# A macaron block on one core: two quarters of the heads in one step of values, tile work placed beside tile work, the last linear as a line of its own

## The chip, the core and the metric

The kernel runs on one core of a Trainium2 chip. The metric is the device time of one execution in microseconds; three runs of the kernel before took 934.36 to 934.98, with a median of 934.62. The engines named below are TensorE (PE for its matmuls, PEld for its loads of weights), VectorE (DVE), ScalarE (ACT), GpSimd (POOL) and SyncE (SP, a DMA queue). Everything is in fp32 but for one masking product in bf16.

## What is computed

The input x has 16 batches of 256 tokens with 128 features. Six sublayers follow, each adding to x; `ln` is a layer norm.

```python
x = x + 0.5 * ffn(ln(x))          # layer 0
x = x + nonlocal_attn(ln(x))      # layer 0, no softmax
x = x + 0.5 * ffn(ln(x))          # layer 0, the same weights
x = x + 0.5 * experts(ln(x))      # layer 1: x + sum over 2 of 8 rank-64 experts, gated by token 0
x = x + attention(ln(x))          # layer 1: 16 heads of 8, rotary, causal softmax
x = x + 0.5 * experts(ln(x))      # layer 1

def ffn(x):                       # all weights ternary with a scale per output
    h = silu(x @ w1) * (x @ w2)   # 128 -> 512
    h = gelu(h @ h1); h = gelu(h @ h2)   # 512 -> 512
    return h @ w3                 # 512 -> 128
```

## The kernel before

The batches are split into nine groups: seven of two batches (four tiles of 128 tokens) and two of one. Everything stays on the chip between the first load of x and its store.

**The planner.** The order of instructions is made while the program is built. Each piece of work is a generator, a *line*, that yields steps; a step (L235 `step`) has an engine, a guessed duration, the PSUM banks and buffers that it takes and drops, the keys that it needs and those that it sets. `begin` (L1004) works out when the next step of a line could start on the planner's clocks; the loop at L1137 takes the earliest, gathers those of the same engine that could start within SLACK of it, and issues the first by a key (L1143): on TensorE the main line comes last while `back` is true (L1142: until the last HURRY feed-forwards have begun), and first after that; then by rank. `issue` (L1053) emits the step's instructions; each engine then runs its own list in that order and waits at semaphores. On TensorE, `issue` adds SWITCH to the guess where `tiles` changes, and `awake` puts matmuls of the identity by itself into waits, but only after `ended` is set. A softmax's exponential is held back by PATIENCE (L1016) while ACT has another function's table loaded. `ended` also decides between two forms of the layer norm (L306) and between masking the scores on VectorE or by TensorE (L769).

**Main line.** `feed_forwards` (L1108) runs the 18 feed-forwards one after another, (0, g) being the group's first and (1, g) its second, in the order of L1103; the last three are (0, 8), (1, 7), (1, 8). After (0, g) it spawns the nonlocal attention, after (1, g) the chain experts, attention, experts. When the last feed-forward has issued its last step, `ended` is set (L1126). A feed-forward (`ffn`, L281) is two products with the 512-wide first linears, two 512 x 512 linears as seven half-size products each (a Strassen form with sums on DVE and POOL, at L478), and the last linear with w3s (L521 to L540), whose steps are part of the main line.

**Attention.** The 16 heads lie in four quarters j of four heads, one in each 32-row strip of the array. For a batch, `maxima` (L760) takes the row maxima of the scores; `weighted` (L825) then, for j in 0, 2, 1, 3, computes scores again (a block of matmuls on 32 rows each, "row" tiles, tile name `pb<-qkv`), spawns `softmax` (an exponential on ACT into one of three buffers `pr`, then two selects on POOL that clear the masked half), and the values line (L881) multiplies by V and a column of ones: a block of 16 matmuls into 32 columns each ("col" tiles, `pb<-pr,vm`), which frees its `pr`. In a block four matmuls run side by side, and it is one step of the planner. In the last two groups (`late`) the two halves of the heads have an output each; otherwise one output follows the fourth quarter.

Of the kernel before, what the change touches and what calls it, by code (L numbers as in the profile page):

```python
# [20 lines left out]
P = 128  # L21
# [6 lines left out]
LANDING = 2.2  # L28
LOAN = 1.5
SPARED = 0.5  # L30
PATIENCE = 1.5
HURRY = 1
SLACK = 0.02
HOP = {"PE": 0.24, "ACT": 0.15, "DVE": 0.12, "POOL": 0.08}
SWITCH = 0.1
# [22 lines left out]
def macaron_kernel(ctx: ExitStack, tc: tile.TileContext, a: dict, out: bass.AP):  # L58
# [316 lines left out]
    def ffn(which, t0, n):  # L375
# [77 lines left out]
            add_residual(t0 + i * n // 2, n // 2, po)  # L453

        for c in range(KC):
            r = yield pe(0.215 * n, banks=1, after=0.0, take=("h",) if c == 0 else ())
            h = r[1] if c == 0 else h
            pu = r[0]
            nc.tensor.matmul(pu.t[:, :N], w1T[:, c * P : (c + 1) * P], xnT.t[:, :N], start=True, stop=True)
            sil = sml.tile([P, TG], F32, name="sil", bufs=3)  # L460
            spawn(silu(c, pu, sil))
            (pw,) = yield pe(0.215 * n, banks=1, after=0.0, drop=(xnT,) if c == KC - 1 else ())
            nc.tensor.matmul(pw.t[:, :N], w2T[:, c * P : (c + 1) * P], xnT.t[:, :N], start=True, stop=True)
            spawn(product(c, pw, sil, h))
            if me == (0, 0) and c == 1:
                fold_w3()
        lo, hi = 0, 2 * P
        for l, w in ((1, h1T), (2, h2T)):
            wx, T = extra[l - 1], {}

            def rest(l=l, h=h, T=T):
                yield from sums(l, h, T)

            spawn(rest())
            bk = {}
            nh = None

            for p, b, first, at, second, needs in (  # L478
                (1, "a", w[:, 0:2], lo, (0, 0), has(l, 0, 0) + (("A11", l),)),
                (5, "d", w[:, 0:2], hi, 1, (("T", 1, l, me), ("A", l))),  # L480
                (6, "b", wx[:, 0], 0, 2, (("T", 2, l, me),)),
                (7, "c", wx[:, 1], 0, 3, (("T", 3, l, me),)),
                (2, "a", w[:, 2:4], lo, (1, 0), has(l, 1, 0) + (("P1", l, me),)),
                (3, "d", wx[:, 2], 0, (1, 1), has(l, 1, 1) + (("V", l, me),)),
                (4, "c", w[:, 2:4], hi, 4, (("T", 4, l, me), ("C22", l, me))),
            ):
                new = p in (1, 5, 6, 7)
                for o in range(2):
                    for k in range(2):
                        begins, ends = o + k == 0, o + k == 2  # L490
                        drop = ()
                        if ends and p in (5, 7, 4):
                            drop = (T[{5: 1, 7: 3, 4: 4}[p]],) + ((h,) if p == 4 else ())
                        r = yield pe(
                            0.1075 * n, banks=int(new and begins), after=0.0, take=("h",) if p == 1 and begins else (),
                            needs=needs, drop=drop, sets=(("P6", l, me),) if p == 6 and ends else (),
                        )
                        if new and begins:
                            bk[b] = r[0]
                        if p == 1 and begins:  # L500
                            nh = r[1]
                        src = block(h, *second) if type(second) is tuple else T[second].t[:, :, :M]
                        nc.tensor.matmul(
                            in_two(bk[b])[:, o, :], first[:, k, at + o * P : at + o * P + P], src[:, k, :],
                            start=new and begins, stop=p in (2, 3, 4, 6) and k == 1, skip_group_check=True,
                        )
                if p == 1:
                    spawn(left(l, bk["a"], nh))
                elif p == 6:
                    spawn(shared(l, bk["b"], bk["d"], nh))  # L510
                elif p == 7:
                    spawn(last_block(l, bk["c"], nh))
                elif p == 2:
                    spawn(gelu(l, 0, 0, in_two(bk["a"]), block(nh, 0, 0), drop=(bk["a"],)))
                elif p == 3:
                    spawn(other_block(l, 0, 1, bk["d"], nh))
                elif p == 4:
                    spawn(other_block(l, 1, 0, bk["c"], nh))
            h = nh

        half = n // 2  # L521
        po = {}
        up, down = (0, 1, 2, 3), (2, 3, 0, 1)
        for t, ks in [(t, down) for t in range(half, n)] + [(t, up) for t in range(half)]:
            new = t in (0, half)
            last = t in (half - 1, n - 1)
            r = yield pe(
                0.225 * len(ks), banks=int(new), after=0.0, needs=tuple((2, i, t // half, me) for i in range(2)),
                drop=(h,) if t == half - 1 else (),
            )  # L530
            if new:
                po[t // half] = r[0]
            b = po[t // half]
            for k in ks:
                nc.tensor.matmul(
                    b.t[:, t % half * P : (t % half + 1) * P], h.t[:, k, t * P : (t + 1) * P], w3s[:, k, :],
                    start=(k == ks[0]), stop=(k == ks[-1]),
                )
            if last:
                spawn(residual(t // half, b))  # L540


    eye, tri = (wgT[:, i * P // 2 : (i + 1) * P // 2].bitcast(BF16) for i in range(2))
# [8 lines left out]
    def nonlocal_attn(t0, n):  # L552
# [17 lines left out]
            copy(m[:, :nb], pp[:, :nb])  # L570
            return m

        gram = yield from product(0.45 * nb, None, None, "gram", (xn,))
        m = yield from product(0.22 * nb, gram, pht, "gph")
        m = yield from product(0.22 * nb, m, wgT, "eff")
        if t0 == 2 * FIRST[NG - 1]:
            spawn(for_the_mask())
        (po,) = yield pe(0.45 * nb, banks=1, drop=(xnT,))
        for t in range(n):
            nc.tensor.matmul(  # L580
                po.t[:, t * D : (t + 1) * D], xnT.t[:, t * P : (t + 1) * P], m[:, t // 2, :], start=True, stop=True
# [4 lines left out]

    def gated(nb, cls):

        (bk,) = yield pe(0.22 * nb, banks=1)
        pl = bk.t[:, : nb * NE].rearrange("p (b e) -> p b e", e=NE)  # L590
        for b in range(nb):
            nc.tensor.matmul(pl[:, b, :], cls[:, b, :].to_broadcast([P, P]), wrT, start=True, stop=True)
# [32 lines left out]
        (bk,) = yield pe(0.23 * nb, banks=1, drop=(ab,))  # L625
# [12 lines left out]
    def applied(key, sg, xnT):  # L638
        yield step(None, 0.0, needs=(key,))
        we = merged[key]  # L640
        (po,) = yield pe(0.225 * sg.n, banks=1, drop=(we, xnT) if sg.last else (xnT,))
# [61 lines left out]
    def attention(sg):  # L703
# [5 lines left out]
        xnT = yield from by_feature(n, xn)  # L709
        if sg.first:  # L710

            (bk,) = yield pe(0.22 * nb, banks=1)
# [32 lines left out]

        spawn(keys())
        spawn(queries())
        (bk,) = yield pe(0.225 * n, banks=1, needs=(("q", sg.t0),), drop=(xnT,))
# [76 lines left out]
        def weighted(i):  # L825
# [55 lines left out]
            def values():  # L881

                po = [None, None]
                for j in (0, 2, 1, 3):
                    new = j == 0 or (late and j == 1)
                    yield step(None, 0.0, needs=(("pr", sg.t0, i, j), ("v", sg.t0)))
                    pr = prs[j]
                    r = yield pe(0.025 + 0.00174 * o, banks=int(new), tiles="col", drop=(pr,))
                    if new:
                        po[j % 2 :] = [r[0]] * (2 - j % 2)  # L890
                    half = slice((j % 2) * w, (j % 2) * w + w)
                    pp = po[j % 2].t[:, half]
                    for k, f, at in runs:
                        for r in range(4):
                            nc.tensor.matmul(
                                pp[32 * r : 32 * r + 32, (f - q0) * P :], vm.t[:, base // P + k, r, j, :],
                                pr.t[:, r, at : at + (q1 - f) * P],
                                start=(j < 2 and k == 0), stop=(j >= 2 and k == q1 - 1), skip_group_check=True,
                            )
                    if late and j >= 2:  # L900
                        spawn(output(pp, oT[:, half], w // 32, j % 2, po[j % 2], ("oT", sg.t0, i, j)))
# [206 lines left out]
    def feed_forwards():  # L1108

        for which, sg in order:  # L1110
# [12 lines left out]
                spawn(chain(experts(sg), attention(sg), after_attention(sg)), (1, sg.g))  # L1123
            if (which, sg) == order[0]:
                fold_rest()
        ended[0] = True  # L1126

    def told(*key):
# [8 lines left out]
    while lines:  # L1137
# [2 lines left out]
        engine = min(ready, key=lambda r: r[:2])[2].next["engine"]  # L1140
        soon = [r for r in ready if r[0] <= t + SLACK and r[2].next["engine"] == engine]
        back = engine == "PE" and begun[0] <= len(order) - HURRY  # L1142
        line = min(soon, key=lambda r: ((r[2] is main) == back, r[2].rank, r[1]))[2]  # L1143
        issue(line)
        if line.over:
            lines.remove(line)
# [69 lines left out]
```

## Time and profile before

| | us |
|---|---|
| median of three runs | 934.62 |
| profiled execution, device time | 934.55 |
| its span on the core | 932.8 |
| PE busy | 904.2 (6524 matmul records) |
| DVE busy | 636.3 |
| ACT busy | 471.5 (110.3 of it 86 loads of tables) |
| POOL busy | 356.4 |
| granted TensorE clock | 0.996 |

The span runs from the first to the last instruction; the device time holds a little more. An fp32 matmul is two records (two passes). In the profile all kernel instructions carry line 227, that of the helper which records them, so groups are told apart by their tiles: `pb` is PSUM, `w3s` the last linear's weights, `T`, `h`, `hS`, `h1T` and `h2T` belong to the 512 x 512 linears, `qkv` to scores, `pr,vm` to values, `ident` alone to the filling matmuls, `wgT` alone (bf16) to the mask on TensorE. A shape such as 128\*32 is rows by columns of the array that a matmul uses.

### The profile page before, as it was taken

What the parts mean: (1) busy time and instruction counts of PE and PEld (TensorE: products, weight loads), DVE (VectorE), ACT (ScalarE), POOL (GpSimd) and SP (SyncE); (2) the same over time, 40 slices, a digit from 0 to 9 for tenths busy, and PEclk for the clock granted to TensorE, in tenths of its full rate; (3) what the DMA queues carried; (4) which work ended last, traced back from release to release, by engine and by line L of the source; (5) the groups of instructions that cost most, each with busy time, mean ns of one, the idle gap of its engine ahead of it and who ended that gap; (6) DMA issues with size and microseconds to landing.
All of it is one profiled execution on the core that took longest, in us unless ns stands there. A gap on an engine that the chain in (4) does not pass through costs nothing.

```text
span 932.8 us, 16458 instructions
## 1 busy us (share of the span) xinstructions
PE 904.2 (97%) x6524; PEld 680.5 (73%) x6524; DVE 636.3 (68%) x1474; ACT 471.5 (51%) x691; POOL 356.4 (38%) x537
## 2 busy tenths in 40 slices
PE   6999999999999999999999999999999989999998
PEld 4778778686786767787677767866786767877666
DVE  4744646875488485894678764894778586977773
ACT  2233533645754646546555466547574657465332
POOL 5311313522454334442453324532463246443441
PEclk9999999999999999999999999999999999999999
DMA  8100000000000000000000000000000000000000
GB/s 240 33 1 1 1 1 12 12 1 1 13 12 12 1 2 12 24 1 1 12 1 24 1 1 13 24 1 1 13 2 23 1 12 1 25 7 2 13 19 12
DMA packets 14588, 13.68 MB, mean 15 GB/s; under 512 B 2032, under 2 KB 11952, under 8 KB 14512
## 3 DMA queue, kind: packets, MB, share of 16 engines
q1 hardware_dynamic: 12496, 8.04, 3.0%
q0 software_dynamic: 1600, 4.20, 1.6%
q8 instruction: 51, 0.84, 0.4%
q10 hardware_dynamic: 416, 0.39, 0.1%
q14 instruction: 25, 0.20, 0.1%
HBM read 10.53 MB, written 2.10 MB: 14 GB/s over the span
## 4 chain that ended last, share of the span: by engine, by line
PE 70%; DVE 14%; ACT 6%; issue 4%; POOL 2%; DMA 2%; SPq 1%; POOLq 0%; DVEq 0%
PE pb L227 70%; DVE mx L227 4%; DVE h L227 3%; ACT L227 2%; ACT pr L227 2%; DVE pb L227 2%; DMA w3s<-in_w3T_dram 1%; ACT h L227 1%; POOL pr L227 1%; DVE T L227 1%; DMA x<-in_x_dram 1%; DVE st L227 1%; DVE qkv L227 1%; POOL rstd L227 1%; DVE row L227 0%
## 5 line engine op out<-in xcount | busy, mean ns | idle before, releaser
L227 DVE TENSOR_TENSOR h<-h,pb 128x512 f32<-128x512 f32 (+1 forms) x180 | 111.7, 620 | 80.8 <-PE pb L227 78.8
L227 PE MATMUL pb<-T,hS 128*128 128x256 f32 (+1 forms) x576 | 131.8, 364 | 3.9 <-DVE h L227 2.8
L227 POOL TENSOR_SCALAR_AFFINE_SELECT pr<-pr 128x512 f32<-128x512 f32 x128 | 78.8, 639 | 140.4 <-ACT pr L227 135.3
L227 ACT ACTIVATE h<-h 128x512 f32<-128x512 f32 (+1 forms) x108 | 62.3, 581 | 137.7 <-DVE h L227 137.3
L227 ACT ACTIVATE pr<-pb 128x1536 f32<-128x1536 f32 x64 | 92.7, 1449 | 54.0 <-PE pb L227 40.4
L227 PE MATMUL pb<-qkv 32*128 32x256 f32 (+2 forms) x1536 | 115.2, 406 | 4.7 <-ACT pr L227 2.5
L227 ACT ACT_TABLE_LOAD x86 | 110.3, 1283 | 17.8 <-PE pb L227 15.5
L227 DVE TENSOR_REDUCE mx<-pb 128x8 f32<-128x2048 f32 (+1 forms) x64 | 111.9, 1750 | 6.1 <-PE pb L227 5.7
L227 PEld LDWEIGHTS pb<-T,hS 128*128 128x128 f32 x576 | 96.5, 190 | 21.1 <-issue 8.6
L227 DVE TENSOR_TENSOR pb<-pb,causal 128x1024 f32<-128x1024 f32 x56 | 68.7, 1226 | 45.4 <-PE pb L227 37.3
L227 PEld LDWEIGHTS pb<-qkv 32*128 32x128 f32 x1536 | 68.0, 184 | 38.3 <-issue 11.4
L227 ACT ACTIVATE xn<-x,shift,rstd 128x128 f32<-128x128 f32 x138 | 57.1, 482 | 52.9 <-POOL shift L227 52.7
L227 POOL TENSOR_SCALAR nm<-mv 128x4 f32<-128x4 f32 (+3 forms) x56 | 14.8, 264 | 168.3 <-DVE mv L227 167.1
L227 POOL TENSOR_TENSOR T<-h 128x512 f32<-128x512 f32 (+1 forms) x48 | 53.4, 1112 | 58.9 <-ACT h L227 54.9
L227 POOL TENSOR_TENSOR T<-h,T 128x512 f32<-128x512 f32 (+1 forms) x40 | 46.1, 1151 | 64.9 <-DVE h L227 35.0
L227 PE MATMUL pb<-xnT,w1T 128*128 128x512 f32 (+1 forms) x144 | 68.9, 560 | 0.9 <-ACT xnT L227 0.9
L227 PE MATMUL pb<-xnT,w2T 128*128 128x512 f32 (+1 forms) x144 | 68.2, 555 | 1.0 <-ACT sil L227 0.8
L227 PE MATMUL pb<-h,h1T 128*128 128x256 f32 (+1 forms) x288 | 68.8, 364 | 0.0
L227 POOL TENSOR_TENSOR rstd<-ve,mhalf 128x4 f32<-128x4 f32 (+3 forms) x63 | 58.9, 935 | 24.9 <-DVE ve L227 20.1
L227 PE MATMUL pb<-h,h2T 128*128 128x256 f32 (+1 forms) x288 | 67.1, 364 | 0.0
L227 PE MATMUL pb<-T,h1T 128*128 128x256 f32 (+1 forms) x288 | 66.1, 359 | 0.0
L227 PEld LDWEIGHTS pb<-w3s,h 128*128 128x128 f32 x512 | 60.6, 192 | 7.0 <-issue 6.0
(138 smaller groups left out, 1568.9 us busy)
## 6 DMA issues: line engine op xcount, KB each, us to landing
out_dram<-x SPq DMA_DIRECT2D x7, 256.0 KB, 2.3
x<-in_x_dram SPq DMA_DIRECT2D x6, 256.0 KB, 5.3
h1T<-in_h1T_dram SPq DMA_DIRECT2D x1, 1024.0 KB, 9.6
h2T<-in_h2T_dram SPq DMA_DIRECT2D x1, 1024.0 KB, 11.0
ab<-in_eab_dram,at POOLq DMA_INDIRECT x32, 2.9
x<-in_x_dram SPq DMA_DIRECT2D x3, 128.0 KB, 5.4
w1T<-in_w1T_dram SPq DMA_DIRECT2D x1, 256.0 KB, 3.5
w2T<-in_w2T_dram ACTq DMA_DIRECT2D x1, 256.0 KB, 3.9
```

Source lines behind the costliest of these rows:

```text
L227: return lambda *args, **kw: tc.keep_in_program_order(getattr(self.engine, name)(*args, **kw))
```

## The change

It has five parts, and touches no arithmetic.

1. `values`: outside the last two groups the quarters (0, 2) are one step and (1, 3) another, each needing both softmaxes and dropping both buffers; the last two groups keep a step per quarter.
2. The planner's choice has a new first key: on TensorE, when the last issued step was in tiles, steps in tiles come ahead of others that could start within SLACK.
3. The last linear of a feed-forward becomes a line of its own, spawned by the main line, which goes on to the next feed-forward. `feed_forwards` waits for both residual sums of the last one before it sets `ended`.
4. HURRY goes from 1 to 2: the main line has TensorE first in the last two feed-forwards. PATIENCE goes from 1.5 to 2.5.
5. Guessed durations of TensorE's steps: 0.015 us more on each product of a feed-forward, 0.237 us for each 128 x 128 matmul where 0.22 to 0.23 stood.

```diff
-PATIENCE = 1.5
-HURRY = 1
+PATIENCE = 2.5
+HURRY = 2
...
-            r = yield pe(0.215 * n, banks=1, after=0.0, take=("h",) if c == 0 else ())
+            r = yield pe(0.015 + 0.215 * n, banks=1, after=0.0, take=("h",) if c == 0 else ())
...
-                            0.1075 * n, banks=int(new and begins), after=0.0, take=("h",) if p == 1 and begins else (),
+                            0.015 + 0.1075 * n, banks=int(new and begins), after=0.0, take=("h",) if p == 1 and begins else (),
...
+        def last_linear(h=h):
...
-            r = yield pe(
-                0.225 * len(ks), banks=int(new), after=0.0, needs=tuple((2, i, t // half, me) for i in range(2)),
...
+                r = yield pe(
+                    0.237 * len(ks), banks=int(new), after=0.0, needs=tuple((2, i, t // half, me) for i in range(2)),
...
+        spawn(last_linear(), since=0.0)
...
-                for j in (0, 2, 1, 3):
-                    new = j == 0 or (late and j == 1)
-                    yield step(None, 0.0, needs=(("pr", sg.t0, i, j), ("v", sg.t0)))
-                    pr = prs[j]
-                    r = yield pe(0.025 + 0.00174 * o, banks=int(new), tiles="col", drop=(pr,))
+                for js in ((0,), (2,), (1,), (3,)) if late else ((0, 2), (1, 3)):
+                    new = js[0] == 0 or (late and js[0] == 1)
+                    yield step(None, 0.0, needs=tuple(("pr", sg.t0, i, j) for j in js) + (("v", sg.t0),))
+                    r = yield pe(
+                        (0.025 + 0.00174 * o) * len(js), banks=int(new), tiles="col", drop=tuple(prs[j] for j in js)
+                    )
...
+        yield step(None, 0.0, needs=tuple(("ffn", h, (1, order[-1][1].t0)) for h in range(2)))
         ended[0] = True
...
-        line = min(soon, key=lambda r: ((r[2] is main) == back, r[2].rank, r[1]))[2]
+        inside = engine == "PE" and tiles[0] is not None
+        line = min(
+            soon, key=lambda r: (inside and r[2].next["tiles"] is None, (r[2] is main) == back, r[2].rank, r[1])
+        )[2]
```

More of the change, by code (lines that the diff above doesn't have):

```diff
@@ L461, in ffn @@
             spawn(silu(c, pu, sil))
-            (pw,) = yield pe(0.215 * n, banks=1, after=0.0, drop=(xnT,) if c == KC - 1 else ())
+            (pw,) = yield pe(0.015 + 0.215 * n, banks=1, after=0.0, drop=(xnT,) if c == KC - 1 else ())
             nc.tensor.matmul(pw.t[:, :N], w2T[:, c * P : (c + 1) * P], xnT.t[:, :N], start=True, stop=True)
@@ L519, in ffn @@
             h = nh
[L521 to L526, printed above, removed]
-            r = yield pe(
-                0.225 * len(ks), banks=int(new), after=0.0, needs=tuple((2, i, t // half, me) for i in range(2)),
[L529 to L537, printed above, removed]
-                )
-            if last:
-                spawn(residual(t // half, b))
+        def last_linear(h=h):
+            half = n // 2
+            po = {}
+            up, down = (0, 1, 2, 3), (2, 3, 0, 1)
+            for t, ks in [(t, down) for t in range(half, n)] + [(t, up) for t in range(half)]:
+                new = t in (0, half)
+                last = t in (half - 1, n - 1)
+                r = yield pe(
+                    0.237 * len(ks), banks=int(new), after=0.0, needs=tuple((2, i, t // half, me) for i in range(2)),
+                    drop=(h,) if t == half - 1 else (),
+                )
+                if new:
+                    po[t // half] = r[0]
+                b = po[t // half]
+                for k in ks:
+                    nc.tensor.matmul(
+                        b.t[:, t % half * P : (t % half + 1) * P], h.t[:, k, t * P : (t + 1) * P], w3s[:, k, :],
+                        start=(k == ks[0]), stop=(k == ks[-1]),
+                    )
+                if last:
+                    spawn(residual(t // half, b))
+        spawn(last_linear(), since=0.0)
     eye, tri = (wgT[:, i * P // 2 : (i + 1) * P // 2].bitcast(BF16) for i in range(2))
@@ L571, in product @@
             return m
-        gram = yield from product(0.45 * nb, None, None, "gram", (xn,))
-        m = yield from product(0.22 * nb, gram, pht, "gph")
-        m = yield from product(0.22 * nb, m, wgT, "eff")
+        gram = yield from product(0.475 * nb, None, None, "gram", (xn,))
+        m = yield from product(0.237 * nb, gram, pht, "gph")
+        m = yield from product(0.237 * nb, m, wgT, "eff")
         if t0 == 2 * FIRST[NG - 1]:
             spawn(for_the_mask())
-        (po,) = yield pe(0.45 * nb, banks=1, drop=(xnT,))
+        (po,) = yield pe(0.475 * nb, banks=1, drop=(xnT,))
         for t in range(n):
@@ L587, in gated @@
     def gated(nb, cls):
-        (bk,) = yield pe(0.22 * nb, banks=1)
+        (bk,) = yield pe(0.237 * nb, banks=1)
         pl = bk.t[:, : nb * NE].rearrange("p (b e) -> p b e", e=NE)
@@ L624, in gated @@
             scaled_by(ab.t[:, b, D:], ab.t[:, b, D:], gw[:, b : b + 1])
[L625 removed]
+        (bk,) = yield pe(0.237 * nb, banks=1, drop=(ab,))
         pw = bk.t[:, : 2 * D].rearrange("p (b d) -> p b d", b=2)
@@ L640, in applied @@
         we = merged[key]
-        (po,) = yield pe(0.225 * sg.n, banks=1, drop=(we, xnT) if sg.last else (xnT,))
+        (po,) = yield pe(0.237 * sg.n, banks=1, drop=(we, xnT) if sg.last else (xnT,))
         for t in range(sg.n):
@@ L710, in attention @@
         if sg.first:
-            (bk,) = yield pe(0.22 * nb, banks=1)
+            (bk,) = yield pe(0.237 * nb, banks=1)
             py = bk.t[:1, : 2 * D].rearrange("p (b d) -> p b d", b=2)
@@ L747, in attention @@
         spawn(queries())
-        (bk,) = yield pe(0.225 * n, banks=1, needs=(("q", sg.t0),), drop=(xnT,))
+        (bk,) = yield pe(0.237 * n, banks=1, needs=(("q", sg.t0),), drop=(xnT,))
         pv = bk.t.rearrange("p (t d) -> p t d", d=D)
@@ L883, in values @@
                 po = [None, None]
-                for j in (0, 2, 1, 3):
-                    new = j == 0 or (late and j == 1)
-                    yield step(None, 0.0, needs=(("pr", sg.t0, i, j), ("v", sg.t0)))
-                    pr = prs[j]
-                    r = yield pe(0.025 + 0.00174 * o, banks=int(new), tiles="col", drop=(pr,))
-                    if new:
[L890 to L899, printed above, removed]
+                for js in ((0,), (2,), (1,), (3,)) if late else ((0, 2), (1, 3)):
[3 more added lines that the diff above has]
+                        (0.025 + 0.00174 * o) * len(js), banks=int(new), tiles="col", drop=tuple(prs[j] for j in js)
+                    )
+                    h = js[0] % 2
+                    if new:
+                        po[h:] = [r[0]] * (2 - h)
+                    half = slice(h * w, h * w + w)
+                    pp = po[h].t[:, half]
+                    for j in js:
+                        for k, f, at in runs:
+                            for r in range(4):
+                                nc.tensor.matmul(
+                                    pp[32 * r : 32 * r + 32, (f - q0) * P :], vm.t[:, base // P + k, r, j, :],
+                                    prs[j].t[:, r, at : at + (q1 - f) * P],
+                                    start=(j < 2 and k == 0), stop=(j >= 2 and k == q1 - 1), skip_group_check=True,
+                                )
+                    j = js[-1]
@@ L900, in values @@
                     if late and j >= 2:
-                        spawn(output(pp, oT[:, half], w // 32, j % 2, po[j % 2], ("oT", sg.t0, i, j)))
+                        spawn(output(pp, oT[:, half], w // 32, h, po[h], ("oT", sg.t0, i, j)))
                     elif j == 3:
```

## The prediction

> **What bounds the kernel now.** I read the page first: busy time by engine, then the slices.
>
> ```profile
> span 932.8 us, 16458 instructions
> PE 904.2 (97%) x6524; PEld 680.5 (73%) x6524; DVE 636.3 (68%) x1474; ACT 471.5 (51%) x691; POOL 356.4 (38%) x537
> ```
>
> TensorE is busy 97% of the span; no other engine is near. A busy PE is not yet a PE at its peak, so I ask next where it waits: the busy times by stage, and TensorE's own waits between the start-up and the last feed-forward.
>
> ```profile
> core 0: us, PE busy (x) PEld busy (x) DVE busy (x) ACT busy (x) POOL busy (x), PEclk, DMA share, GB/s
> 50.00:640.00 590.00, 588.78 (x3851) 437.43 (x3850) 397.98 (x905) 309.84 (x456) 216.00 (x312) 1.00 0.03 7
> 640.00:845.50 205.50, 197.34 (x1685) 156.04 (x1684) 148.92 (x351) 121.29 (x181) 88.35 (x140) 1.00 0.03 10
> 845.50:932.80 87.30, 77.65 (x833) 56.34 (x831) 59.51 (x162) 26.82 (x34) 31.03 (x48) 0.98 0.04 12
> ```
>
> The columns after the stretch are its length and the busy us of PE, PEld, DVE, ACT and POOL. From 50 to 640 us PE idles 1.2 us; from 640 to 845.5 us 8.2 us; the last matmul of the last feed-forward (w3s) starts at 845.2. So up to 845 us the end is set by how much TensorE is given to do: an instruction less there is time less. The last 87 us are a tail: the last attentions, a chain across engines, with 90 matmuls of the identity by itself (180 records) that fill PE's waits.
>
> The third view is PE's timeline, for what work in tiles costs. A row is a stretch of like matmuls; what counts is the distance from one start to the next, since the ends overlap.
>
> ```profile
> 255.14 1.05 PE L227 MATMUL pb<-we,xnT 128*128 128x128 f32 x8
> 256.12 0.86 PE L227 MATMUL pb<-pr,vm 128*32 128x256 f32 x16
> 256.91 1.56 PE L227 MATMUL pb<-T,h1T 128*128 128x256 f32 x6
> ...
> 834.99 1.95 PE L227 MATMUL pb<-T,hS 128*128 128x128 f32 x16
> 836.87 0.94 PE L227 MATMUL pb<-qkv 32*128 32x256 f32 x16
> 837.74 0.86 PE L227 MATMUL pb<-pr,vm 128*32 128x256 f32 x16
> 838.53 1.16 PE L227 MATMUL pb<-h,h2T 128*128 128x128 f32 x8
> ```
>
> Every matmul leaves two records. In this trace whole-array records start 0.112 us (128 columns), 0.216 (256) or 0.429 us (512) apart, and four tile matmuls run side by side in the time of one. A block of values (pr,vm, 128*32) is two groups of 256 columns and two of 128, ideally 2 x 0.216 + 2 x 0.112 = 0.656 us. It takes 0.79 from its start to the next (256.12 to 256.91), and starts 0.08 later than the eight records before it need (255.14 + 0.90 = 256.04). Over the 54 value blocks between whole-array work the median, measured from the end of that work's own 0.112 or 0.216, is 0.88: **0.23 us of switching each**. A block of scores (qkv, 32*128) of the same columns takes 0.96: **0.31**. At 836.87 scores are followed at once by values; the scores still take 0.87, as they do ahead of whole-array work, but the values' entry of some 0.1 us is gone.
>
> **The change, part by part.** For what a scheduler decides I laid the two programs' instructions side by side and counted.
>
> *Values of two quarters together* (all but the last two groups): up to the last w3s matmul there are 50 value blocks before and 24 after (two quarters slip behind it). 26 x 0.23 = 6.0 us off PE. The pair waits for both probability tiles; queued behind that wait on PE is whatever the planner put next, and the three pr buffers come free in pairs. A quarter needs 1.45 us of Exp and 2 x 0.64 of selects. A group of two batches has eight quarters and two feed-forwards; w3s rows end at 227.6, 281.8 and 335.6 us, so in 108 us, and each of three buffers may be held 3 x 108 / 8 = 40 us, far over the 5 us or so (0.96 + 1.45 + 1.28 + 0.88) that a quarter needs; I take this wait as covered by feed-forward matmuls, at nothing. If not, 24 pairs x (1.45 + 1.28 + 0.3 of hops) = 73 us at the very worst, below nothing not at all.
>
> *Tiles next to tiles* (the new first key of the choice): direct neighbours of scores and values go from 6 to 8 before the last w3s and from 4 to 8 behind it: 2 x 0.1 = 0.2 and 4 x 0.1 = 0.4 us. The Trainium skill (TensorEngine Tiling (Array Packing), Key Properties) says that changing the tiling mode drains TensorE, which would make scores to values as dear as scores to whole array plus whole array to values, and this part worth nothing. The row above shows one entry saved, so I take the 0.1; by the rule the sum is 0.6 less.
>
> *The last linear as its own line, main first in the last two feed-forwards (HURRY 2), ended set later*: these move work. Ahead of the last w3s go away, besides the two quarters' values (2 x 0.656 = 1.3 us): score matmuls, 4 of 512 columns, 8 of 256 and 8 of 128 (fours side by side, two records each: 2 x 0.429 + 4 x 0.216 + 4 x 0.112 = 2.2 us), in three blocks (3 x 0.31 = 0.9); two transposes come (+0.45). All of that is done in the tail instead.
>
> Sum up to the last w3s: -6.0 - 0.2 - 1.3 - 2.2 - 0.9 + 0.4 (rounded) = **-10.2 us**, so it starts near 835.0.
>
> *Waits that stay.* Gaps of PE over the normal spacing add to about 10 us between 640 and 845.5, the longest this:
>
> ```profile
> 759.50 1.06 PE L227 MATMUL pb<-T,hS 128*128 128x128 f32 x8
> 762.73 1.13 PE L227 MATMUL pb<-T,hS 128*128 128x128 f32 x8 [2.17 <-DVE h L227]
> ```
>
> A one-batch feed-forward's next product waits for a DVE sum (0.41 us) that stood behind two mask additions of 1.23. In the new order the feed-forward before the last has almost no attention work between its products (about 19 us of PE where 28 were), so such waits lose cover there; but nothing of the kind then stands in DVE's way either. I keep the 10 us, with -3 and +6 as ends.
>
> *The planner's other numbers* (0.237 for 0.22, 0.015 on each product, PATIENCE 2.5) add no instruction; they act through the order counted here. ScalarE gets 9 more table loads (1.283 each, 11.5 us) and 25 more scalings that VectorE loses (some 0.5 each): about 24 us on an engine at 51%. Covered while PE has other work; ends 0 and +3. The DMAs on SP and POOL's gathers are as many as before.
>
> *The tail.* It keeps 87.3 us by its chain; what changes: 13 Exps become 15 and one more step of scores is masked by TensorE (8 bf16 matmuls, four in 0.53 us: +1.1), PE gets the 4 us of moved work, and loses 22 identity matmuls (22 x 0.224 = -4.9), two value blocks (-0.5), one score block (-0.3), four entries (-0.4) and a pair of transposes (-0.4). PE's stream is 1.9 us shorter. VectorE loses about 4 us of small work to the others and to the earlier part. The chain is of the same steps, the last scores and Exps included. I take **-1.0**, ends -3 and +5.
>
> The identity matmuls have a second use. The Trainium skill (TensorE: Matmul & The Clock Gate, the closing table) says that only idle gaps over about 3 us bring the clock down to half; then 22 fewer cost nothing, as no gap in the trace reaches that. The trace disagrees:
>
> ```profile
> 905.00:908.20 3.20, 1.21 (x18) 0.76 (x11) 2.79 (x3) 1.82 (x2) 1.06 (x2) 1.00 0.00 0
> 908.20:911.70 3.50, 3.50 (x27) 1.96 (x28) 1.60 (x2) 0.00 (x0) 0.17 (x1) 0.51 0.00 0
> ```
>
> A stretch with 1.21 of 3.20 us busy was followed by one at clock 0.51. That halving costs 3.5 x 0.5 = 1.7 us; the new order has a stretch without fill at the same place, so I keep one, and put a second (+1.7) inside the tail's upper end.
>
> Total: 932.8 - 10.2 - 1.0 = 921.6 us of span. The profiled execution took 934.55, 1.75 more than its span, and lies 0.07 under the median of the runs; so **923.4 us**.
>
> **The rivals.**
> - *Forecast* (0.65): the switches and the moved work come off, the tail holds: 919 to 927.
> - *Thin feed-forward* (0.15): main first strips the one-batch feed-forwards of cover, and 4 to 7 us of waits like the 2.17 above return: 927 to 931. For it: nearly all gaps lie in this part; against: in the first two feed-forwards, which also run bare, PE does not idle (50 to 640: 1.2 us in all), though with twice the columns.
> - *Tail as it was or longer by the work moved* (0.07): two quarters in a row behind the last feed-forward, each 0.96 + 1.45 + 1.28 + 0.88 = 4.6 us, end in series: 923.4 + 1.0 + 9.2 = 933.6: no change.
> - *Slower* (0.11): buffers. The pair's first pr is held until the second's selects are done; the fourth quarter's scores take that buffer, and PE's order has them ahead of other work. It turns the result when more than 11.2 / 24 = 0.47 us a pair is uncovered; at 0.9 us a pair, 923.4 + 24 x 0.9 = 945. Against it: PE waits on pr for 2.1 us in all from 50 to 845.5, and the 40 us a buffer may be held.
> - The better end (0.02): waits vanish too, under 919.
>
> **How the numbers follow.** What a measurement of this kernel can tell from no change is about 0.2%, 1.9 us. Faster: 0.65 + 0.15 + 0.02 and a little of the third case, 0.83; same 0.06; slower 0.11. The range leaves out the slower rival and most of the third: 918.5 to 931.
>
> **What would show it.** In the changed profile: PE's records almost as many (about 44 fewer identity records, 16 more for masks), value blocks of x32 with the next start some 1.45 us on instead of 2 x 0.88 + work between; the last w3s near 835; from 50 to 640 us PE still idle for about 1 us. Wrong if PE waits on ACT pr or POOL pr grow by over 5 us (buffers), if gaps on DVE h or ACT h between 750 and 835 grow (thin feed-forward), if w3s ends by 835 and the span is still over 925 (tail).

## The result

| | before | after |
|---|---|---|
| median of the runs, us | 934.75 (11 runs, 932.60 to 936.19) | 936.73 (11 runs, 935.62 to 938.19) |
| profiled execution: span, us | 932.8 | 934.2 |
| last w3s matmul starts, us | 845.2 | 848.6 |
| from there to the end, us | 87.6 | 85.6 |

The ratio is 1.0023, with a 95% interval of 1.0013 to 1.0032: slower by about 2 us, where 11 us less were forecast. The page of the changed kernel begins:

```profile
span 934.2 us, 16434 instructions
PE 894.9 (96%) x6488; PEld 678.7 (73%) x6488; DVE 652.5 (70%) x1461; ACT 490.3 (52%) x720; POOL 341.1 (37%) x530
```

TensorE is busy 9.3 us less in a span that is 1.4 us longer. By stage (length, then busy us of PE, PEld, DVE, ACT, POOL):

```profile
50.00:640.00 590.00, 581.07 (x3848) 434.01 (x3848) 417.38 (x912) 317.53 (x462) 201.48 (x301) 1.00 0.03 7
640.00:849.00 209.00, 199.06 (x1629) 160.41 (x1622) 147.06 (x347) 125.80 (x195) 84.77 (x138) 1.00 0.03 9
849.00:934.20 85.20, 74.40 (x863) 54.07 (x861) 58.16 (x147) 33.45 (x43) 33.85 (x55) 0.99 0.05 13
```

From 50 to 640 us, where PE idled 1.2 us, it now idles 8.9. TensorE's timeline shows gain and loss side by side:

```profile
541.12 1.03 PE L227 MATMUL pb<-T,hS 128*128 128x256 f32 x4
542.08 1.15 PE L227 MATMUL pb<-qkv 32*128 32x256 f32 x16
543.16 1.51 PE L227 MATMUL pb<-pr,vm 128*32 128x256 f32 x32
544.59 1.13 PE L227 MATMUL pb<-T,hS 128*128 128x256 f32 x4
547.10 1.13 PE L227 MATMUL pb<-T,hS 128*128 128x256 f32 x4 [1.38 <-DVE h L227]
```

Two quarters of values (x32) take 1.43 us from start to next start, where two blocks took 2 x 0.79 and an entry of some 0.1 each after whole-array work. Two rows on, TensorE stands still for 1.38 us until a sum on VectorE is done. TensorE's waits from 50 to 640 us, first before, then after (us in total, times, longest):

```profile
PE pb L227 <- ACT pr L227: 0.7, 4, 0.2
PE pb L227 <- DVE mx L227: 0.5, 1, 0.5
```

```profile
PE pb L227 <- DVE h L227: 4.8, 5, 1.4
PE pb L227 <- DVE xn L227: 2.0, 3, 0.8
PE pb L227 <- ACT pr L227: 0.8, 3, 0.4
```

The releasers are the feed-forward's sums on VectorE (h) and the layer norm's output (xn), not the probabilities (pr).

**Two sums for every run below.** *Counted* is TensorE's work up to the last w3s matmul: the order of the program, with the distances of starts from the trace of before (0.112, 0.216 and 0.429 us a record; entry into tiles 0.096, leaving scores 0.22, leaving values 0.147). *Rest* is the start of the last w3s in the trace less this count: start-up, stretches at half the clock, and all waits, also those too short to show as idle. A gain of work shows in the first, a loss by waiting in the second. Only differences between rows can be read: the count takes a transpose for two records, as the prediction does, while the traces show one (192 records `ident,xn` for 192 transposes, 0.109 us apart). With 198 to 204 transposes ahead of the last w3s, each count is some 22 us too high and each rest as much too low; a difference between rows moves by less than 1 us.

| run | time against before, us | counted | last w3s | rest | PE idle 50 to 640 | tail |
|---|---|---|---|---|---|---|
| before | | 821.4 | 845.2 | 23.9 | 1.2 | 87.6 |
| after | 936.73, +2.0 | 811.0 | 848.6 | 37.6 | 8.9 | 85.6 |
| e1 after, old times | 943.41, +8.5 | 801.8 | 840.2 | 38.5 | 6.1 | 106.2 |
| e2 before, new times | 955.12, +20.3 | 824.3 | 875.3 | 51.0 | 8.7 | 79.6 |
| e3 before, pairs | 936.80, +1.9 | 813.6 | 843.1 | 29.5 | 3.0 | 92.0 |
| e4 after, no own line | 943.55, +8.7 | 810.8 | 851.3 | 40.5 | 10.7 | 89.1 |
| e5 pairs, plan frozen | 943.42, +8.6 | 815.6 | 853.5 | 38.0 | 9.4 | 86.6 |
| e6 before, SLACK nudged | 942.22, +7.4 | 822.0 | 848.9 | 26.8 | 1.3 | 91.6 |
| e7 after, no mask sums | 928.16, -6.7 | 811.0 | 842.3 | 31.4 | 7.5 | 84.2 |
| e8 before, no mask sums | 929.40, -5.5 | 821.4 | 840.9 | 19.5 | 0.7 | 87.0 |
| e9 after, light VectorE | 925.72, -9.4 | 811.0 | 840.9 | 30.0 | 7.1 | 82.4 |
| e10 before, light VectorE | 922.81, -12.3 | 821.4 | 838.0 | 16.6 | 0.0 | 83.1 |
| e11 after, quarters apart | 949.85, +14.7 | 808.7 | 842.3 | 33.5 | 8.2 | 106.8 |
| e12 pairs, replanned | 934.64, -0.5 | 810.2 | 836.2 | 26.0 | 5.0 | 95.5 |
| e13 before, PATIENCE 2.5 | 945.99, +11.0 | 818.1 | 853.1 | 35.0 | 3.1 | 91.8 |
| e14 before, SPARED 0.52 | 936.26, +1.3 | 820.6 | 847.1 | 26.5 | 2.3 | 87.8 |
| e15 pairs, replanned | 933.45, -1.8 | 808.0 | 834.4 | 26.4 | 2.6 | 95.9 |
| e16 pairs, replanned | 933.46, -1.8 | 809.0 | 833.5 | 24.5 | 4.4 | 96.8 |

Times are medians; each difference is to the median of before that was run with it (934.75 to 935.28). The other columns are of the one execution that was traced; that of e1 was the slowest of its four (948.23, at a granted clock of 0.979; the others took 940.86 to 945.65), so its rest and its tail are longer than those of a typical run. Between before and after the work falls by 10.4 us, close to the 10.2 of the prediction, and the rest grows by 13.7. So the question is where 13.7 us of waits come from.

### The profile page after: what moved, and what is told of

Same layout as the page of the kernel before. It is cut to its first block, busy times and chain, and to the rows that moved or that the text cites. A ratio compares the mean times of both kernels' runs of the same rounds, so it can differ in the third digit from the quotient of the medians.

```text
span 934.2 us, 16434 instructions
## 1 busy us (share of the span) xinstructions
PE 894.9 (96%) x6488; PEld 678.7 (73%) x6488; DVE 652.5 (70%) x1461; ACT 490.3 (52%) x720; POOL 341.1 (37%) x530
## 4 chain that ended last, share of the span: by engine, by line
PE 69%; DVE 15%; ACT 5%; issue 5%; POOL 3%; DMA 2%; SPq 1%; POOLq 0%; DVEq 0%; ACTq 0%
PE pb L227 69%; DVE mx L227 3%; DVE pb L227 3%; DVE h L227 2%; ACT pr L227 2%; ACT L227 1%; ACT xn L227 1%; DMA w3s<-in_w3T_dram 1%; DVE xn L227 1%; POOL pr L227 1%; POOL rstd L227 1%; DVE rot L227 1%; DVE T L227 1%; DVE den L227 1%; DVE st L227 1%
## 5 line engine op out<-in xcount | busy, mean ns | idle before, releaser
L227 PE MATMUL pb<-T,hS 128*128 128x256 f32 (+1 forms) x576 | 127.5, 362 | 7.7 <-DVE h L227 5.4
L227 PE MATMUL pb<-qkv 32*128 32x256 f32 (+2 forms) x1536 | 118.7, 405 | 8.3 <-ACT pr L227 4.5
L227 ACT ACTIVATE pr<-pb 128x1536 f32<-128x1536 f32 x64 | 92.7, 1449 | 30.6 <-PE pb L227 29.4
L227 DVE TENSOR_TENSOR pb<-pb,causal 128x1024 f32<-128x1024 f32 x54 | 66.3, 1227 | 24.7 <-PE pb L227 21.9
L227 DVE TENSOR_TENSOR x<-x,pb 128x256 f32<-128x256 f32 (+2 forms) x79 | 37.1, 473 | 59.4 <-PE pb L227 59.0
L227 PE MATMUL pb<-T,h2T 128*128 128x256 f32 (+1 forms) x288 | 66.7, 362 | 0.2 <-POOL T L227 0.2
L227 PE MATMUL pb<-h,h1T 128*128 128x256 f32 (+1 forms) x288 | 66.1, 361 | 0.4 <-DVE x L227 0.4
L227 PE MATMUL pb<-h,h2T 128*128 128x256 f32 (+1 forms) x288 | 64.6, 359 | 0.0
## 6 DMA issues: line engine op xcount, KB each, us to landing
h2T<-in_h2T_dram SPq DMA_DIRECT2D x1, 1024.0 KB, 10.8
```

Source lines behind the costliest of these rows:

```text
L227: return lambda *args, **kw: tc.keep_in_program_order(getattr(self.engine, name)(*args, **kw))
```

## The experiments

Four theories were set against each other. V: the pairs themselves, since a step now waits for two softmaxes and holds two buffers. G: the new guessed times. L: the last linear's own line. N: none of them in particular; any edit makes the planner draw a new order, and the kernel before has a good one. D, added later: the new order overloads VectorE's queue.

**e1, the changed kernel with the old guessed times.**

```diff
-            r = yield pe(0.015 + 0.215 * n, banks=1, after=0.0, ...
+            r = yield pe(0.215 * n, banks=1, after=0.0, ...
```

(and so for each of the new times)

> The changed kernel with the old guessed durations of TensorE's steps. Counted from the order of its instructions with the distances of the trace, TensorE has 869.5 us to do without the fill (changed kernel 866.1, before 871.5). If the raised times are what makes TensorE wait (theory G: the planner thinks TensorE later than it is, and puts its next product too close behind the sums that it needs), waits from 50 to 640 us fall from some 9 us to about 1, and the time is 923 to 927. If the pairs of quarters make the waits (theory V), or the last linear's own line (theory L), it stays at 934 to 938.

Measured 943.41 (ratio 1.0082, 1.0051 to 1.0114), slower than the changed kernel and outside both answers. Idle time from 50 to 640 falls only to 6.1, and the rest stays at 38.5, though some 7 us of it are two stretches at half the clock (13.6 us). The last w3s comes 8.4 us earlier, since less work lies ahead of it; the tail grows to 106.2 us, with 67.7 us of TensorE's counted work in it (55.1 in the changed kernel, 50.1 before) and two more such stretches. The new times alone do not explain the changed kernel: without them most of its waits stay.

**e2, the kernel before with the new guessed times alone** (the reverse of that edit).

> The kernel before with only the new guessed durations. TensorE's work without fill is counted at 871.2 us, as before. Theory G: waits from 50 to 640 us rise from 1 to 8 us or more, the time to 942 to 947. Theories V and L: waits as before, 933 to 937.

Measured 955.12 (1.0215, 1.0195 to 1.0234). The work counted is the same in all to 0.4 us; the rest up to the last w3s grows by 27.1:

```profile
50.00:640.00 590.00, 581.32 (x3791) 428.81 (x3793) 418.81 (x927) 305.25 (x435) 201.49 (x298) 1.00 0.03 7
640.00:875.50 235.50, 218.61 (x1817) 171.18 (x1810) 158.02 (x360) 132.88 (x197) 100.00 (x155) 0.98 0.03 8
```

PE idles 8.7 us in the first stretch and 16.9 in the second. Some 5 of the 27.1 us are no wait: three stretches after 640 us, 10.2 us in all, ran at half the clock. Numbers that exist only in the planner cost 20 us. Taken by itself this fits G (8 us or more of waits; its 942 to 947 is exceeded). But in e1 the same numbers are gone and most waits stay, so what they do depends on the order that they are put into.

**e3, the kernel before with pairs of quarters alone.**

```diff
-                for j in (0, 2, 1, 3):
+                for js in ((0,), (2,), (1,), (3,)) if late else ((0, 2), (1, 3)):
```

> The kernel before with only the pairs of quarters in one values step. TensorE's work without fill is counted at 866.7 us, 4.8 less than before (fewer switches, some more masks in the tail). Theory V: waits from 50 to 640 us rise by 8 us or more and the time is 935 to 942. Theories G and L: waits as before, 926 to 931.

Measured 936.80 (1.0019, 1.0009 to 1.0028). The time is in V's range, the idle time between the two answers (3.0 us, neither 1 nor 9); there is no gain. Of the work up to the last w3s 7.8 us go, the last w3s comes only 2.1 earlier, and the tail takes 4.4 more.

**e4, the changed kernel without the own line.**

```diff
-        spawn(last_linear(), since=0.0)
+        yield from last_linear()
```

> The changed kernel with the last linear's steps in the main line again. TensorE's work without fill is counted at 866.5 us, as in the changed kernel (866.1). Theory L (the own line goes ahead of all else and takes banks that scores want): the waits go, 922 to 927. Theories G and V: 933 to 938.

Measured 943.55 (1.0100, 1.0078 to 1.0122), outside both answers and with more idle time than with the line (10.7 us). L falls.

**e5, pairs in the plan of the kernel before.** The planner issues every step as before; only the matmuls of the first quarter are held until the second's step.

```diff
+                    if not late and j < 2:
+                        waiting = (pr, block)
+                        late_work.append(waiting)
+                    else:
+                        if not late and waiting in late_work:
+                            late_work.remove(waiting)
+                            waiting[1]()
+                        block()
```

> The kernel before with its plan kept step for step: the planner still sees a values step per quarter, but outside the last two groups the first quarter's matmuls are emitted only with those of the second (or earlier, if another step takes its buffer). 26 value blocks merge; TensorE's work without fill is counted at 865.3 us, 6.2 less than before. Theory N (a new plan costs waits of its own, whatever it was made for; the pairs themselves cost none): waits as before, 927 to 930. Theory V (the pair's wait for both softmaxes holds TensorE): 934 or more.

Measured 943.42 (1.0100, 1.0081 to 1.0118), V's answer. Its waits from 50 to 640 us:

```profile
PE pb L227 <- ACT pr L227: 4.8, 12, 0.5
PE pb L227 <- DVE oT L227: 2.9, 4, 0.7
PE pb L227 <- DVE mx L227: 0.5, 1, 0.5
```

Here the pairs do cost what V says: scores wait for exponentials (0.7 us before), and the output product for an attention output that comes later (none before). N's forecast for this run was wrong: in an order made for quarters, a pair has a price. But these two rows are not the changed kernel's (0.8 and none): its new order avoids them and meets others.

**e6, a nudge that means nothing to the chip.**

```diff
-SLACK = 0.02
+SLACK = 0.03
```

> The kernel before with SLACK 0.03 for 0.02, a nudge that means nothing for the hardware: a part of the steps changes places, the work stays (872.1 us without fill, before 871.5). Theory N: waits grow and the time is 938 to 950. If waits come only from what the change's parts do (V, L or G), it stays at 933 to 936.

Measured 942.22 (1.0073, 1.0057 to 1.0090), as N says. The stretch from 50 to 640 is as before (1.3 us idle); 3.7 us come before the last w3s and 4 in the tail, where the clock was at half for 10.2 us in all (3.4 before; the last 3 us of either span, also at half, are left out).

**e7 and e8, both kernels without the mask sums ahead of the maxima.**

```diff
-                    nc.vector.tensor_tensor(
-                        d, d, causal.unsqueeze(1).unsqueeze(1).to_broadcast([P, 4, 2, P]), ALU.add
-                    )
```

> The changed kernel, every instruction in the same order on every engine, but the additions of the causal mask ahead of the row maxima are left out (54 on VectorE, 66 us; the maxima then see masked places too). Theory D (VectorE's queue is what the new order runs into: sums that TensorE needs stand behind long work there): TensorE's waits from 50 to 640 us fall from 8.9 to 2 or less and the time falls by 15 us or more, to under 922. If TensorE waits on the order of other engines, it falls by no more than the kernel before does in the next run.

> The kernel before with the same additions left out (56 on VectorE, 69 us). It idles 1.2 us from 50 to 640 and 8.2 from there to the last feed-forward's end, of which some 4 follow VectorE. Theory D: 5 to 10 us less, 925 to 930, so that the changed kernel is then the faster of the two by 5 to 10 us, as the prediction's sum for TensorE's work has it. Otherwise both fall alike and stay within 3 us.

Measured 928.16 and 929.40. The changed kernel gains 8.6 on its own time, the one before 5.5; so the changed one gained more than e7's last sentence allowed, but it is now only 1.2 faster, no 5 to 10. Its idle time from 50 to 640 us stays at 7.5.

**e9 and e10, the same with maxima over an eighth of the columns too.**

```diff
-                    nc.vector.tensor_reduce(to[:, :, 1 - v], sc[:, :, 2 * n : 2 * n + 2, :], AX.X, ALU.max, negate=True)
+                    nc.vector.tensor_reduce(to[:, :, 1 - v], sc[:, :, 2 * n : 2 * n + 2, : w // 8], AX.X, ALU.max, negate=True)
```

> The changed kernel in its own order on every engine, without the mask additions (66 us of VectorE) and with the row maxima over an eighth of their columns (112 us of VectorE become some 15 to 20). Left out: masks of the maxima and most of their columns; the scores, softmax and all of TensorE's work stay. Theory D (TensorE's new waits are for VectorE's queue): TensorE's idle time from 50 to 640 us falls from 8.9 us to 2 or less, and the time is 5 to 10 us under that of the next run. Theory N in the form that the order on TensorE, ScalarE and GpSimd makes the waits too: idle time stays over 5 us, and the two are within 3 us.

> The kernel before with the same left out. Its stretch from 50 to 640 us has no wait to lose (1.2 us); it gains from 640 us on: 918 to 926.

Measured 925.72 and 922.81: the kernel before gains more, and the changed one still idles 7.1 us although VectorE is busy 326 us of the 590 instead of 417. The rest falls by 7.6 in the one and 7.3 in the other, so 13.4 of the 13.7 us between them stay. D falls. One place shows why. First the changed kernel, then e9 (which runs some 2 us ahead), without the rows of weight loads; PE, DVE and POOL in order of time:

```profile
433.81 1.26 POOL L227 TENSOR_TENSOR T<-h,T 128x512 f32<-128x512 f32 x1 [2.72 <-issue]
...
435.54 1.13 PE L227 MATMUL pb<-T,hS 128*128 128x256 f32 x4
435.91 1.20 DVE L227 TENSOR_TENSOR pb<-pb,causal 128x1024 f32<-128x1024 f32 x1
437.02 0.67 DVE L227 TENSOR_TENSOR h<-h,pb 128x512 f32<-128x512 f32 x1
...
437.75 0.70 PE L227 MATMUL pb<-T,hS 128*128 128x256 f32 x2 [1.08 <-DVE h L227]
```

```profile
433.86 1.13 PE L227 MATMUL pb<-T,hS 128*128 128x256 f32 x4
435.03 1.41 DVE L227 TENSOR_TENSOR h<-h,pb 128x512 f32<-128x512 f32 x2 [2.18 <-PE pb L227]
435.77 0.92 PE L227 MATMUL pb<-T,hS 128*128 128x256 f32 x3 [0.78 <-DVE h L227]
```

In e9 VectorE had been idle for 2.18 us and began its sum as soon as TensorE's product was out; TensorE still waits 0.78. What it waits for is a PSUM bank (a piece of TensorE's output memory). In the kernel's program the waiting product writes the bank that the product just before it filled and that this sum reads, so it is held until the sum is done; its own input T was written well before. So the distance between two users of a bank on TensorE's list is too short, whatever the length of VectorE's list. In the trace of before such products have a block of scores or values between them: near 460 us the list goes T,hS x2, pr,vm, T,hS x2, qkv, T,hS x2. Three of the changed kernel's five waits on h between 50 and 640 us are of this kind, with the earlier product directly ahead (at 327.4, 437.8 and 547.1 us: 3.5 of the 4.8 us). Counted on the lists of the same stretch, the products of the 512 x 512 linears take a bank again after at least 1.3 us of other TensorE work in the kernel before; in the changed one five do so after less than 1 us, these three after none; in e15, whose pairs wait little, the least is 2.2. The other waits of the 13.7 us were not traced one by one.

**e11, the changed kernel with quarters apart.**

```diff
-                for js in ((0,), (2,), (1,), (3,)) if late else ((0, 2), (1, 3)):
+                for js in ((0,), (2,), (1,), (3,)):
```

> The changed kernel with a values step per quarter again, all its other parts kept. TensorE's work without fill is counted at 875.7 us, 9.6 more than in the changed kernel. Theory N: the pairs are worth their work even so, 940 to 950. Theory V: the waits go with the pairs and the time stays within 3 us of the changed kernel's.

Measured 949.85 (1.0151, 1.0136 to 1.0166). Idle time stays at 8.2 without any pair, so such waits do not need pairs, and V's answer is missed. But e11 draws a new order too: its last w3s comes 6.3 us earlier than the changed kernel's, and all of the loss lies in the tail (21.2 us more), which has 67.0 us of counted work and 10.2 us at half the clock besides the end of the span. What the pairs are worth in one and the same order this run can't say.

**e13 and e14, two edits of one number of the planner in the kernel before.**

```diff
-PATIENCE = 1.5
+PATIENCE = 2.5
```

```diff
-SPARED = 0.5
+SPARED = 0.52
```

> The kernel before with PATIENCE 2.5 alone, one number of the change that adds and removes no instruction of TensorE but fill and masks. TensorE's work without fill is counted at 870.8 us (before 871.5). Theory N, in which every edit draws a new order and the kernel before has an unusually good one: waits from 50 to 640 us over 3 us, the time 941 to 952. If the order as such does not matter and waits come from the pairs, the own line or the new times alone, 933 to 937.

> The kernel before with SPARED 0.52 for 0.5, which is no part of the change and means nothing for the hardware, but moves the steps of the steady stretch too (the nudge of SLACK moved those from 640 us on alone). TensorE's work without fill is counted at 870.8 us. Theory N: waits from 50 to 640 us rise from 1.2 to 4 to 9 us, 938 to 947. Otherwise 933 to 937.

Measured 945.99 (1.0113, 1.0096 to 1.0130) and 936.26 (1.0010, 0.9998 to 1.0022). The first is as N says, though more of it lies after 640 us than was expected. Its kernel holds one thing more of the change, the later setting of `ended`, which alters the order behind the last w3s only: so the last w3s, 7.9 us later, is PATIENCE's doing, while for the 4.2 us of longer tail the two are not told apart. The second is not clear of no change and less than N's 938 to 947: an edit is not always dear. Its rest is 2.6 us more, its work 0.8 less.

**e12, e15 and e16, the pairs in orders drawn again.** Old guessed times, pairs, own line, no tile key, HURRY 1, and other values of four planner numbers, picked by the planner's own clock. For e15:

```diff
-PATIENCE = 2.5
-HURRY = 2
-SLACK = 0.02
-SPARED = 0.5
-LOAN = 1.5
+PATIENCE = 1.6
+HURRY = 1
+SLACK = 0.01
+SPARED = 0.4
+LOAN = 2.0
```

> Pairs of quarters and the last linear's own line, with the old guessed times, the old order of choice, HURRY 1, PATIENCE 2.0, SPARED 0.6, LOAN 2.0: of 146 such settings the one whose order leaves TensorE's list shortest on the planner's own clock. TensorE's work without fill is counted at 865.8 us, 5.7 less than before. Theory N (a setting is drawn anew with every edit, and the kernel before is a good draw): with a draw as good, 927 to 932. Theory V: over 934, since the pairs are in it.

> As e12 (pairs, own line, old guessed times, HURRY 1), with PATIENCE 1.6, SLACK 0.01, SPARED 0.4, LOAN 2.0, the draw with the least planned idle time on TensorE from 50 to 640 us. TensorE's work without fill is counted at 866.8 us, 4.7 less than before, and 808.0 up to the last w3s (before 821.4). Theory N: idle time from 50 to 640 us under 4 us, the last w3s at 832 to 836; what is left goes to the tail, where 5 us more work lies: 929 to 936 in all. Theory V (pairs cost waits as such): last w3s no earlier than 842.

> As e12 with PATIENCE 1.75, SLACK 0.025, SPARED 0.6, LOAN 1.5, the draw with the shortest list on the planner's clock in a second search. TensorE's work without fill is counted at 865.3 us, and 809.0 up to the last w3s. Theory N: last w3s at 834 to 838, 929 to 936. Theory V: last w3s no earlier than 842.

Measured 934.64 (0.9989, 0.9979 to 0.9998), 933.45 (0.9975, 0.9962 to 0.9987) and 933.46 (0.9979, 0.9969 to 0.9988). e12 misses N's 927 to 932 and lies just where V put it, over 934; the other two fall within N's 929 to 936 and beat the kernel before by 1.8 us, with the last w3s far ahead of V's 842. For e15 by stage:

```profile
50.00:640.00 590.00, 587.36 (x3851) 442.62 (x3850) 422.84 (x935) 308.75 (x451) 190.78 (x288) 1.00 0.03 7
640.00:836.00 196.00, 187.35 (x1618) 151.98 (x1616) 146.22 (x359) 110.81 (x162) 82.05 (x131) 1.00 0.03 9
836.00:930.30 94.30, 82.01 (x910) 59.31 (x906) 63.04 (x162) 32.10 (x40) 34.85 (x55) 1.00 0.04 13
```

The pairs are in, PE idles 2.6 us from 50 to 640, and the last w3s starts at 834.4, 10.8 earlier than before. VectorE is busier here (423 us) than in the changed kernel (417), which speaks once more against D. What is left of the gain shrinks in the tail: 58.8 us of TensorE's counted work lie behind the last w3s (before 50.1), and the tail takes 8.3 us more.

## Why the prediction was wrong

- **What bounds the kernel: this is the step that failed.** "An instruction less there is time less" took the stretch from 50 to 640 us as one without waits, and kept "PE still idle for about 1 us" for the new order. TensorE was not held by its work alone: it hardly waited in the order that it had. The prediction read the absence of waits as a property of the stage; it was one of that order.
- **The price of switching: right.** Merged blocks take 1.53 us from the end of the work before, two blocks took 2 x 0.88: 0.23 a pair, as estimated. Counted work up to the last w3s fell by 10.4 against 10.2 forecast. (The two transposes of that sum cost 0.22 us and not 0.45, since each is one record.)
- **Waits that stay: this is the term that was missed.** "I keep the 10 us, with -3 and +6 as ends" is about the stretch from 640 us on; for the one before it nothing was allowed. Gaps over the normal spacing, summed the same way, went from 10.0 to 13.6 us between 640 and the last w3s, which is within these ends, and from 1.5 to 11.8 between 50 and 640, which had none: +13.9 in all, and the rest grew by 13.7. So the last w3s came at 848.6 instead of 835.0. The view on TensorE's list was used to count instructions and not to ask what stands between a product and the next one that takes its bank or needs its result.
- **The planner's other numbers.** "They add no instruction; they act through the order counted here" was true, and it was the reason to look, not to leave them: in the kernel before, the new times alone cost 20 us, and PATIENCE alone moved the last w3s by 7.9 us with 3.3 us less work ahead of it. Both are waits for the most part, beside 10.2 and 3.4 us at half the clock.
- **The tail: near, by luck in part.** It fell by 2.0 (forecast 1.0). But the halving of the clock kept in it, priced at 1.7, did not come (the granted clock stayed whole until 931.9 us), so without that the tail was 0.3 shorter. Its list of terms also adds up to -1.4 and not to the -1.9 that it gives. And work moved behind the last w3s is not free in general: with 56 to 59 us of it the tail took 95 to 97 in e12, e15 and e16.
- **The rivals.** The slower one named buffers. TensorE's waits on pr up to the last w3s were to grow by over 5 us; they went from 2.1 to 1.5, so the kernel is slower (by 2 us, where that rival had 10) without that cause, though in the frozen order (e5) waits of that kind were real. The thin feed-forward came too: the longest single wait of the changed kernel between 50 us and the last w3s is there, 1.69 us on ACT sil at 789 us, but from 640 us on gaps grew by 3.6 of the 13.9 only.
- **What stays open.** That waits of the new order took the gain is shown: work fell by 10.4 and the rest grew by 13.7; edits that leave the work as it is cost 7 to 20 us (e2, e6, e13), if not every time (e14); and pairs stand in an order with 2.6 us of idle time (e15) as in one with 8.9. Which rule of the planner brings the waits was not found. Taking out the times, the own line or the pairs leaves the rest at 38.5 (some 7 of it at half the clock), 40.5 and 33.5, beside 37.6, and each is slower; the tile key and HURRY were not run alone. That the kernel before is an unusually good draw is argued, not measured: of three one-number edits two were slower and one was not clear of no change, and two orders drawn anew with pairs were 1.8 us faster than it.

## What to carry to other kernels

Where a planner or a list fixes the order on in-order engines, a change has two prices, the work it removes and the waits of the order that comes with it; on an engine that is 97% busy the second can be the larger, and the profile of before can't show it. Count the work from the two lists, then look in the new list for each instruction and the next one that takes its bank or needs its result, and ask whether enough stands between. Measure a neutral nudge before believing a gain of 1%, and draw the order again before giving up a saving that the count shows.

## What the runs showed of the hardware

TensorE's clock was halved without any long gap, and for 6.8 us on end. In e1 (length, then busy us):

```profile
750.20:753.60 3.40, 1.79 (x23) 1.35 (x19) 0.48 (x1) 2.62 (x4) 2.23 (x5) 1.00 0.00 0
753.60:760.40 6.80, 6.80 (x53) 5.33 (x55) 3.04 (x13) 4.86 (x5) 4.92 (x7) 0.50 0.10 32
```

1.6 us of waits in 3.4, none longer than 0.85, were followed by 6.8 us at half the clock, some 3.4 us of work lost. This execution of e1, the slowest of four, had 30.6 us at half clock in four places between 750 and 890 us, up to 15 us of its time; in such an order a wait can cost more than itself. A low busy share was not followed by a halving each time: the changed kernel was busy 1.97 of 3.40 us from 908.4 on, and the clock stayed whole.

A long gap was followed by a halving as well. In its start-up the kernel before waits 4.46 us for `xn` (up to 16.8 us), and from 17.4 to 20.8 us its clock is at half; the prediction's "no gap in the trace reaches that" overlooks it. So the rule that the prediction weighs there fits the start-up; what its own rows of 905 to 911.7 us and those of e1 above contradict is the "only".
